# Two attention layers on one core: variances and row sums by quarters, 1 / sigma through DRAM, and a new order of the second layer's finish

## The chip, the cores and the metric

The kernel runs on one core of a Trainium2 chip. Its time is the device time of one execution in microseconds (us). The engines are TensorE (PE; PEld is its weight load), VectorE (DVE), ScalarE (ACT), GpSimd (POOL) and SyncE (SP), which here only issues DMAs. PE, DVE, ACT and POOL execute in the order in which the program names their instructions, and so does SP's queue.

## The reference

Everything is float32. The input x is [B, C, H, W] = [2, 512, 64, 32], so each batch has 2048 tokens of 512 channels.

```python
# layer 0: attention over all 2048 tokens, 8 heads of 64
q, k = concat(x, emb) @ Wq, concat(x, emb) @ Wk      # emb: 32 rows of frequency, 32 of time
v = x @ Wv
x = x + softmax(q k^T / 8) v @ Wout + bout

# layer 1: Nystrom attention with 256 landmarks, then a linear map
t = tokens(x)
q, k, v = split(layer_norm(t) @ Wqkv)
qL, kL = means of q / 8 and of k over 8 tokens each
attn1 = softmax(q kL^T); attn2 = softmax(qL kL^T); attn3 = softmax(qL k^T)
out = attn1 @ (pinv6(attn2) @ (attn3 @ v)) + conv33(v)   # pinv6: six steps of an iteration
t = t + out @ Wout1 + bout1
t = t + (layer_norm(t) @ nf4_weights^T) @ W^T            # the two maps become one matrix mT
```

`layer_norm` takes the mean and the variance over the 512 channels of each token, with no learned scale.

## The kernel before

Channels lie on the 128 partitions, tokens along the free axis, in four blocks of TB = 512 tokens per batch (`NTB` = 4); heads go in pairs (`NPAIR` = 4 per batch). A matmul of float32 is two instructions.

**Layer 0.** `Heads0` makes queries, keys and values of a pair. For the queries and keys it adds an embedding e, which for batch 0 is computed once on POOL (L889) and written to DRAM for batch 1. `attention0` runs the scores, exponentials, sums and values, and after each group of steps calls `advance` on a list of generators, the filler: the next pair's projections, and the finish of the batch before. A generator that yields `GAP` lets the others pass without having done anything; any other yield is a turn used. `finish0_units` is that finish for batch 0: it loads x, adds the output projection (`out0_units`), and normalizes (`norm0_steps`) for layer 1. Batch 1's finish runs by hand between the first projections of layer 1 (L1801 to L1825), with `others` as the work beside it. There `load_x`, the loads of `xr` (L1795), the stores of keys and queries (L1243) and the weights are all on SP's queue.

**A normalization.** `statistics` is a generator of four steps: the sum of the four channel blocks on DVE; the mean, by a matmul with a constant matrix `mean_w`, and the subtraction on DVE; squares on ACT and their sums on DVE; and the variance, again by a matmul with `mean_w` over all 512 columns (L1000), whose result is the same on all 128 partitions, and Sqrt on ACT. The caller takes the reciprocal over 128x512 on DVE (L1017, L1650) and multiplies.

**Layer 1.** `todo` holds eight pairs, batch 1's first. `attend` and `gram` make attn2 and its Gram matrix. For pair n, `pinv` runs the iteration; between its steps `chunk` (five times) and `last` (six times) are called, which emit pieces of other work: attn3 of the pair after (`attn3_scores`, `landmarks_values`, `start_values`), attn1 of the pair before (`attn1_scores`, `attn1_add`, `attn1_values`, `attn1_sums`, `attn1_inverse`, `attn1_end`), the values of the pair after the next, and `advance(finish)`. attn1's row sums are already made with 32 columns of ones at a time (`sums_of`, L779), each quarter of the partitions for another part of the columns; after a reciprocal over 256 columns, eight DMAs on SP (`spread`, L790) carry them to all columns. attn3's row sums use 64 columns of ones (L1406) and a reciprocal over 256 columns in place.

**The finish of layer 1.** `Finish1` is one block of it: x1 is loaded into `xb` by four DMAs on SP, `out_units` adds the output projection (yp_g, L965, with DVE's residual L972), `steps` or `norm_units` normalize, `map_units` applies mT (fp_g, L1682) and writes out. `finish1_units` strings together batch 1's four blocks on one `xb` buffer, 13 turns each; it is put on the list after pair 4 (`n == NPAIR`). After the last pair, `last_attn1` gives the rest of its attn1 in turns, and a string orders the turns: f is a turn of the finish, 1 one of `last_attn1`, a and b the output units of batch 0's blocks 0 and 1, s and t their normalization steps. Batch 0's four blocks `fs`, with their loads, are made ahead of the string. After it comes the bound's check (`halves`, `bp`, `ok`, `oks`, `bad`, L2051 to L2064), which tells whether the plain exponentials were safe, and then the loop over the last blocks.

[...]From layer 1's pairs on, `bank` has four of them (tag pp), before that two, beside two buffers of two banks each for scores (`scores_bank`).

Of the kernel before, what the change touches and what calls it, by code (L numbers as in the profile page):

```python
# [663 lines left out]
def fast_path(  # L664
# [108 lines left out]
    def sums_of(rs, acc):  # L773


        for h in range(2):
            for j in range(2):
                lo = h * D + j * Q
                nc.tensor.matmul(  # L779
                    rs[lo : lo + Q, :LM], lhsT=ones[:, :Q], rhs=acc[:, h, j * LM : (j + 1) * LM],  # L780
                    start=True, stop=True,
                )

    def spread(dst, few):

        for h in range(2):
            for to in range(2):
                for j in range(2):
                    lo, src = h * D + to * Q, h * D + j * Q
                    nc.sync.dma_start(dst[lo : lo + Q, j * LM : (j + 1) * LM], few[src : src + Q, :])  # L790
# [31 lines left out]
    nc.vector.memset(emb_sb, 0.0)  # L822
# [3 lines left out]
    def load_w0(kind, cols, queue=nc.sync):  # L826
        w = {"q": wq0, "k": wk0}[kind]
        nc.sync.dma_start(w_sb[kind][:, :, cols], chunked(w[:C, cols]))
        queue.dma_start(we[kind][:, cols], w[C:, cols])

    nc.gpsimd.dma_start(emb_sb[:32, :H], freq)
    nc.gpsimd.dma_start(emb_sb[32:, H:], time)
    load_w0("q", slice(0, P), nc.scalar)

# [23 lines left out]
    class Heads0:  # L858
# [12 lines left out]
        def embedded_and_projected(self, kind):  # L871

            cols, xbs = self.cols, self.xbs
            if kind == "q":
                self.q = qopool.tile([P, S], F32, tag="qo", name=f"q_{self.name}")

            def embedded(kind):


                e = wpool0.tile([P, H, W], F32, tag="e", name=f"e_{kind}_{self.name}")  # L880
                flat, kept = e.rearrange("p h w -> p (h w)"), e_d["qk".index(kind), self.hp]
                if self.b:
                    nc.sync.dma_start(flat, kept)
                    return flat
                fp = bank(f"fp_{kind}_{self.name}")
                nc.tensor.matmul(fp[:, : H + W], lhsT=we[kind][:, cols], rhs=emb_sb, start=True, stop=True)
                ft = wpool0.tile([P, H + W], F32, tag="ft", name=f"ft_{kind}_{self.name}")
                nc.vector.tensor_copy(ft, fp[:, : H + W])
                nc.gpsimd.tensor_tensor(  # L889
                    e,  # L890
                    ft[:, :H].unsqueeze(2).to_broadcast([P, H, W]),
                    ft[:, H:].unsqueeze(1).to_broadcast([P, H, W]),
                    ALU.add,
                )
                nc.sync.dma_start(kept, flat)
                return flat

            def project(kind, dst, e, t):
                toks = slice(t * TB, (t + 1) * TB)
                pp = bank(f"pp_{kind}_{self.name}_{t}")  # L900
                for k in range(KC):
                    nc.tensor.matmul(  # L902
                        pp, lhsT=w_sb[kind][:, k, cols], rhs=xbs[t][:, k, :], start=k == 0, stop=k == KC - 1
                    )
                nc.vector.tensor_tensor(dst[:, toks], pp, e[:, toks], ALU.add)  # L905

            dst = self.q if kind == "q" else self.k
            e = embedded(kind)
            if self.b:
                yield from gap(2)  # L910
            else:
                yield
                yield GAP
            for t in range(NTB):
                project(kind, dst, e, t)
                yield
# [63 lines left out]
    def statistics(xb, xn, part, name, squares, row):  # L980
# [12 lines left out]
        for i, other in enumerate(others):  # L993
            nc.scalar.activation(other, xn[:, 2 + i * n : 2 + (i + 1) * n, :], AF.Square)
            to = sq[:, i * n : (i + 1) * n, :]
            nc.vector.tensor_tensor(to, to, other, ALU.add)  # L996
        nc.vector.tensor_tensor(sq[:, 0, :], sq[:, 0, :], sq[:, 1, :], ALU.add)  # L997
        yield
        var = bank(f"var_{name}")
        nc.tensor.matmul(var, lhsT=mean_w, rhs=sq[:, 0, :], start=True, stop=True)  # L1000
        rstd = row()
        nc.scalar.activation(rstd, var, AF.Sqrt, bias=eps, scale=1.0)
# [7 lines left out]
    def norm0_steps(b, t, xb, xn, part):  # L1010
# [6 lines left out]
        nc.vector.reciprocal(rstd, rstd)  # L1017
# [8 lines left out]
    def finish0_units(b, oTs, outs_done):  # L1026
        last = None
        for t in range(NTB):
# [4 lines left out]
            for m, _ in enumerate(out0_units(b, t, xb, oTs)):  # L1033
                if last and m == 0:
                    next(last)
                yield
# [14 lines left out]
            yield  # L1051
        next(last)
# [155 lines left out]
    class Pair:  # L1208
# [59 lines left out]
        def attend(self):  # L1268

            i, L = self.i, self.L  # L1270
            scs = scores_bank(f"sc2_{i}") if i + 1 < NPAIR else None
            X = self.X = [zpool.tile([P, 2, LM + 1], F32, tag=f"M{h}", name=f"X_{i}_{h}") for h in range(2)]
            rs = small.tile([P, 4], F32, tag="rs2", name=f"rs2_{i}")
            for h in range(2):
                nc.gpsimd.memset(X[h][:, :, LM:], 1.0)
            for h in range(2):
                rows_h = slice(h * D, (h + 1) * D)
                sc = scs[:, h, :] if scs is not None else bank(f"sc2_{i}_{h}")
# [122 lines left out]
        def landmarks_values(self):  # L1401

            rs = bank(f"rs3_{self.name}")
            for j in range(2):
                for h in range(2):
                    nc.tensor.matmul(  # L1406
                        rs[h * D : (h + 1) * D, :LM],
                        lhsT=ones,
                        rhs=self.acc3[:, h, j * LM : (j + 1) * LM],
                        start=j == 0,  # L1410
                        stop=j == 1,
                    )
            rinv = self.acc3[:, 0, :]
            yT = rinv[:, LM:]
            nc.scalar.copy(rinv[:, :LM], rs[:, :LM])
            nc.vector.reciprocal(rinv[:, :LM], rinv[:, :LM])
            nc.vector.tensor_tensor(yT, self.av3[:, :LM], rinv[:, :LM], ALU.mult)
            X = exps(f"X2_{self.name}").rearrange("p a b -> p (a b)").rearrange("p (h k n) -> p h k n", h=2, k=2)
            self.X = [X[:, h] for h in range(2)]
            for h in range(2):  # L1420
                nc.sync.dma_start(self.X[h], X_d[self.b, self.hp, h])
            yield
# [205 lines left out]
    class Finish1:  # L1628
# [3 lines left out]
        def __init__(self, b, t, os, xb, xn):  # L1632
            self.b, self.t, self.os, self.xb, self.xn = b, t, os, xb, xn
            self.name = f"g_{b}_{t}"
            toks = slice(t * TB, (t + 1) * TB)
            for m in range(KC):
                nc.sync.dma_start(xb[:, m, :], chunked(x1_d[b])[:, m, toks])
# [4 lines left out]
        def steps(self, row):  # L1642
# [5 lines left out]
            for rstd in statistics(self.xb, self.xn, self.xn[:, :2, :], self.name, squares, row):  # L1648
                if rstd is not None:
                    nc.vector.reciprocal(rstd, rstd)  # L1650
                    self.rstd = rstd
                yield

        def norm_units(self):
            steps = self.steps(lambda: deviation(self.name))
            next(steps)
            yield GAP
            next(steps)
            yield
# [3 lines left out]
            yield  # L1663

# [27 lines left out]
    def finish1_units(b, os):  # L1692
        for t in range(NTB):
            xb = block_of(lpool, "xr", f"xb_g_{b}_{t}")
            f = Finish1(b, t, os, xb, lambda: block_of(lpool, "xn", f"xn_g_{b}_{t}"))
# [125 lines left out]
    advance(more)  # L1821
# [37 lines left out]
    def second_of_first():  # L1859
# [4 lines left out]
        for part in (landmarks, conv, landmarks, start, conv):  # L1864
# [20 lines left out]
    todo[1].prefetch_w()  # L1885
    vals = [values(1)]
    advance(vals)
    for n in todo[NPAIR - 1].front():
        advance(vals, n // 2)
    start_scale()  # L1890
    todo[0].prefetch1(kvpool.tile([P, S], F32, tag="k", name="q2_first"))
# [4 lines left out]
    for n, pair in enumerate(todo):  # L1896
# [20 lines left out]
        def chunk(c):  # L1917
            nonlocal landmarks
            if before and 0 < c <= n_ones:
                before.attn1_end(c - 1)  # L1920
            advance(finish)
# [35 lines left out]
        def last(i):  # L1957
            nonlocal start
            if i == 1 and after:
# [31 lines left out]
        if n == NPAIR:  # L1991
            finish.append(finish1_units(1, [p.o for p in todo[:NPAIR]]))

    def last_attn1():
        pair, ended = todo[-1], []
        for t in range(NTB):
            for j in range(2 if t else 0):
                pair.attn1_scores(t, j)
                if ended:
                    pair.attn1_end(ended.pop())  # L2000
                yield
            pair.attn1_add(t)
# [16 lines left out]
    fs = [last_block(t) for t in range(NTB)]  # L2019

# [5 lines left out]

    outs = [f.out_units() for f in fs]
# [9 lines left out]
    st = [f.steps(deviation_of(t)) for t, f in enumerate(fs)]  # L2037

    ones_last = last_attn1()
    for c in "f1f1f1f1f1f1f1fa1a1a1as11bs1bs1bbt":  # L2040
        if c == "f":
            advance(finish)
        else:
            next({"1": ones_last, "a": outs[0], "b": outs[1], "s": st[0], "t": st[1]}[c])
# [5 lines left out]

    n = 3 * B * NPAIR  # L2051

    halves = row_of("halves_f")[:, :P]
    nc.gpsimd.memset(halves, 0.0)
    nc.gpsimd.memset(halves[:D, :D], 1.0)
    nc.gpsimd.memset(halves[D:, D:], 1.0)
    bp = bank("bp_f")
    nc.tensor.matmul(bp[:, :n], lhsT=halves, rhs=bound, start=True, stop=True)
    ok = small.tile([P, n], F32, name="ok_f")
    nc.vector.tensor_scalar(ok, bp[:, :n], SAFE, None, ALU.is_lt)  # L2060
    oks = small.tile([P, 1], F32, name="oks_f")
    nc.vector.tensor_reduce(oks, ok, AX.X, ALU.min)
    nc.vector.tensor_scalar(oks, oks, -1.0, 1.0, ALU.mult, ALU.add)
    nc.gpsimd.partition_all_reduce(bad, oks, P, bass_isa.ReduceOp.max)  # L2064

# [99 lines left out]
```

## Time and profile before

| | us |
|---|---|
| median of 3 runs (lowest, highest) | 2764.85 (2764.79, 2766.75) |
| the profiled execution, its own time | 2763.73 |
| its span, first to last instruction | 2761.9 |
| PE busy in the span | 2703.8 |
| DVE, ACT, POOL busy | 1629.0, 905.8, 164.7 |

The mean granted clock of TensorE is 0.995 of full. The stages, with the busy time of PE in each, from the table of windows:

| us from the span's start | what | PE busy |
|---|---|---|
| 0 to 45 | loads, first projections | 40.7 |
| 45 to 1380 | layer 0's attention (finish of batch 0 within) | 1326.5 |
| 1380 to 1750 | finish of layer 0's batch 1, layer 1's keys and queries | 363.1 |
| 1750 to 2300 | pairs 0 to 5 | 548.2 |
| 2300 to 2590 | pairs 6 and 7 | 271.9 |
| 2590 to 2672 | rest of attn1, finish | 71.2 |
| 2672 to 2762 | last blocks | 82.1 |

A line of the profile names the engine, the line of the kernel, the operation, what it writes from what it reads, the shape and the count; busy time and idle time follow. In a timeline the first two numbers are the start and the length in us, and a bracket gives how long the engine had been idle before, and what it waited for.

### The profile page before, as it was taken

To read this page: it belongs to the slowest core of one execution; us is meant where nothing else is said; L and a number is where in the kernel's file an instruction comes from. 1 tells how busy PE (TensorE), PEld (TensorE's weight loads), DVE (VectorE), ACT (ScalarE), POOL (GpSimd) and SP (SyncE) were. 2 spreads that over 40 slices of the span, in tenths; PEclk is the share of its full clock that TensorE was granted. 3 is DMA by queue.
4 is the path that set the end of the run, shared out by engine and by line. 5 is a ranking of instruction groups with operands and counts; after the bars stand their busy time and mean duration, and the time that the engine had idled before them with its cause. 6 is when DMAs were issued, how large, how long until landed. Compare 5 with 4: busy or idle time off the path is not lost. (4 is left out here: it accounts for less than half of the span.)

```text
span 2761.9 us, 41236 instructions
## 1 busy us (share of the span) xinstructions
PE 2703.8 (98%) x16994; PEld 1363.3 (49%) x16994; DVE 1629.0 (59%) x2068; ACT 905.8 (33%) x1352; POOL 164.7 (6%) x125
## 2 busy tenths in 40 slices
PE   9999999999999999999999999999999999899898
PEld 5343443434443334343344465777667767555334
DVE  2768787765558756657657444544644545556465
ACT  1434343433335334344512222223332323221210
POOL 1101101000001100000011000000000000000000
PEclk9999999999999999999999999999999999999999
DMA  4100000212111210021035532213111202111301
GB/s 145 42 9 24 28 20 26 83 35 69 32 66 54 96 39 9 21 73 41 24 107 187 187 121 90 95 32 126 43 36 59 81 9 90 40 64 31 107 31 47
DMA packets 112661, 174.00 MB, mean 63 GB/s; under 512 B 16320, under 2 KB 68048, under 8 KB 107856
## 3 DMA queue, kind: packets, MB, share of 16 engines
q1 hardware_dynamic: 107968, 154.46, 17.3%
q0 software_dynamic: 4416, 16.79, 1.6%
q8 instruction: 135, 2.21, 0.3%
q14 instruction: 62, 0.51, 0.1%
q10 hardware_dynamic: 80, 0.03, 0.0%
HBM read 90.87 MB, written 63.57 MB: 56 GB/s over the span
## 5 line engine op out<-in xcount | busy, mean ns | idle before, releaser
L1084 DVE TENSOR_TENSOR acc_f<-acc_f,p_f 128x1024 f32<-128x1024 f32 x448 | 582.6, 1300 | 208.8 <-ACT p_f L1074 180.2
L1074 ACT ACTIVATE p_f<-sc_f 128x1024 f32<-128x1024 f32 x512 | 496.4, 1021 | 564.2 <-PE sc_f L1066 561.5
L1066 PE MATMUL sc_f<-q_f,k_f 64*64 64x512 f32 x4096 | 491.1, 594 | 2.7 <-ACT p_f L1074 2.7
L1096 PE MATMUL av_f<-p_f,v_f 64*64 64x512 f32 x4096 | 484.3, 589 | 0.0
L1096 PEld LDWEIGHTS av_f<-p_f,v_f 64*64 64x64 f32 x4096 | 156.5, 133 | 283.0 <-issue 283.0
L1066 PEld LDWEIGHTS sc_f<-q_f,k_f 64*64 64x64 f32 x4096 | 145.8, 133 | 285.6 <-issue 262.0
L1239 PE MATMUL pp<-xh,w 128*128 128x512 f32 x512 | 231.0, 603 | 0.7 <-ACT q L1242 0.7
L1239 PEld LDWEIGHTS pp<-xh,w 128*128 128x128 f32 x512 | 95.8, 192 | 122.2 <-issue 115.0
L1532 PE MATMUL pb<-R 128*128 128x192 f32 (+1 forms) x640 | 151.1, 383 | 1.6 <-DVE M L1545 1.6
L1532 PE MATMUL pa<-M 128*128 128x192 f32 (+1 forms) x640 | 150.7, 380 | 0.1
L950 PEld LDWEIGHTS vp_f<-wv_f,x 128*128 128x128 f32 x1024 | 115.7, 192 | 13.5 <-issue 11.8
L950 PE MATMUL vp<-w,xh 128*128 128x128 f32 x1024 | 120.8, 276 | 0.0
L950 PEld LDWEIGHTS vp<-w,xh 128*128 128x128 f32 x1024 | 117.0, 192 | 7.2 <-issue 4.2
L1532 PEld LDWEIGHTS pb<-R 128*128 128x128 f32 x640 | 107.7, 192 | 25.1 <-DVE M L1545 2.3
L950 PE MATMUL vp_f<-wv_f,x 128*128 128x128 f32 x1024 | 118.7, 277 | 0.0
L1532 PEld LDWEIGHTS pa<-M 128*128 128x128 f32 x640 | 108.0, 193 | 21.0 <-ACT M L1523 2.5
L902 PE MATMUL pp_q_f<-x,wq_f 128*128 128x512 f32 x256 | 114.4, 599 | 2.1 <-DVE q_f L905 1.4
L965 PE MATMUL yp_g<-o,wo_f 128*128 128x512 f32 x256 | 115.5, 598 | 0.8 <-DVE y_g L1671 0.8
L902 PE MATMUL pp_k_f<-x,wk_f 128*128 128x512 f32 x256 | 114.3, 599 | 1.7 <-DVE k_f L905 1.3
L1682 PE MATMUL fp_g<-xn_g,mT 128*128 128x512 f32 (+1 forms) x264 | 115.7, 589 | 0.0
L965 PE MATMUL yp_f<-q_f,wo_f 128*128 128x512 f32 x256 | 113.7, 598 | 0.9 <-DVE xr_f L972 0.9
L1114 POOL TENSOR_TENSOR q_f<-q_f,rinv_f 128x512 f32<-128x512 f32 x32 | 44.4, 1387 | 1041.9 <-DMA rinv_f<-acc_f 850.7
(196 smaller groups left out, 2719.3 us busy)
## 6 DMA issues: line engine op xcount, KB each, us to landing
xh<-xh_fd SPq DMA_DIRECT2D x12, 1024.0 KB, 5.6
rinv_f<-acc_f SPq DMA_DIRECT2D x256, 32.0 KB, 1.8
xr_f<-in_x_dram SPq DMA_DIRECT2D x8, 1024.0 KB, 5.2
x_fd<-xr_f POOLq DMA_DIRECT2D x8, 1024.0 KB, 5.0
xh_fd<-xn_f POOLq DMA_DIRECT2D x8, 1024.0 KB, 4.6
k_fd<-k SPq DMA_DIRECT2D x32, 256.0 KB, 2.6
q_fd<-q SPq DMA_DIRECT2D x32, 256.0 KB, 3.1
xb_g<-x_fd SPq DMA_DIRECT2D x32, 256.0 KB, 4.2
```

Of the source, the lines that this page charges most:

```text
L902: nc.tensor.matmul(pp, lhsT=w_sb[kind][:, k, cols], rhs=xbs[t][:, k, :], start=k == 0, stop=k == KC - 1)
L950: nc.tensor.matmul(vp[:, j * P : (j + 1) * P], lhsT=xb[:, k, j * P : (j + 1) * P], rhs=w_of(k), start=k == 0, stop=k == KC - 1,)
L965: nc.tensor.matmul(yp, lhsT=wo_sb[:, k, m * P : (m + 1) * P], rhs=oTs[k][:, toks], start=k == 0, stop=k == NPAIR - 1,)
L1066: nc.tensor.matmul(sc[r * D : (r + 1) * D, h, :], lhsT=hd.k[rows, lo : lo + D], rhs=hd.q[rows, t * TB : (t + 1) * TB], start=True, stop=True,)
L1074: nc.scalar.activation(p, sc, AF.Exp, scale=D**-0.5)
L1084: nc.vector.tensor_tensor(acc, first if c == 1 else acc, p, ALU.add)
L1096: nc.tensor.matmul(av[r][half, :], lhsT=hd.v[keys, c, half], rhs=pp[keys, h, :], start=c == 0, stop=c == NST - 1,)
L1114: nc.gpsimd.tensor_tensor(o, o, rinv, ALU.mult)
L1239: nc.tensor.matmul(pp, lhsT=self.w[j][:, c, :], rhs=xhs[t][:, c, :], start=c == 0, stop=c == KC - 1)
L1532: nc.tensor.matmul(dst, lhsT=lhsT[:, k, t * P : (t + 1) * P], rhs=rhs[:, k, :], start=k == 0, stop=k == 1)
L1682: nc.tensor.matmul(fp[:, cols], lhsT=mT[:, k, m * P : (m + 1) * P], rhs=self.xn[:, k, cols], start=k == 0, stop=k == KC - 1,)
```

## The change

**Statistics.** The variance is four matmuls of 128 columns each with 32 columns of `mean_w`, so quarter j of the partitions holds the variances of quarter j of the tokens. Sqrt and the reciprocal work on 128x128. One row of each quarter is written to DRAM (4 x 128) and read back to all partitions as 128x512, both on SP; the reciprocals in the callers go. `apart` puts a step between the squares on ACT and their sums on DVE. In `finish0_units` the multiplication (`next(last)`) moves from the next block's output unit 0 to unit 1, with two gaps ahead of the last one; in the finish by hand two turns instead of one stand ahead of the last.

**attn3's row sums.** `sums_of` takes a number of parts: two parts of 128 columns accumulate, and 128 columns of results are inverted and spread by eight DMAs. The product with the values becomes a step of its own, one step later, called from `last(0)`.

**Order.** Batch 1's finish is put on the list at pair 4's `chunk(1)`. A block of it takes 18 turns: its x1 comes by one DMA on POOL, with two gaps before its first unit; gaps stand behind the steps of its normalization. The string is new and has a letter n, at which batch 0's blocks are made and their 16 loads issued. `attn1_add` is emitted with the scores that it adds. The bound's check moves ahead of the pairs, around `start_scale`.

**Smaller ones.** The embedding's table loads and the first wq go to ACT's queue; the first pair's embedding is added on DVE instead of POOL; in `attend` the two heads' scores are two tiles (two buffers) instead of one, and the memset of ones is on DVE.

```diff
-    def sums_of(rs, acc):
-        for h in range(2):
-            for j in range(2):
-                lo = h * D + j * Q
-                nc.tensor.matmul(
-                    rs[lo : lo + Q, :LM], lhsT=ones[:, :Q], rhs=acc[:, h, j * LM : (j + 1) * LM],
-                    start=True, stop=True,
-                )
+    def sums_of(rs, acc, parts=1):
+        n = TB // parts // 2
+        for part in range(parts):
+            for h in range(2):
+                for j in range(2):
+                    lo, at = h * D + j * Q, part * 2 * n + j * n
+                    nc.tensor.matmul(
+                        rs[lo : lo + Q, :n], lhsT=ones[:, :Q], rhs=acc[:, h, at : at + n],
+                        start=part == 0, stop=part == parts - 1,
+                    )
...
     def load_w0(kind, cols, queue=nc.sync):
-        nc.sync.dma_start(w_sb[kind][:, :, cols], chunked(w[:C, cols]))
+        queue.dma_start(w_sb[kind][:, :, cols], chunked(w[:C, cols]))
...
-    nc.gpsimd.dma_start(emb_sb[:32, :H], freq)
-    nc.gpsimd.dma_start(emb_sb[32:, H:], time)
     load_w0("q", slice(0, P), nc.scalar)
+    nc.scalar.dma_start(emb_sb[:32, :H], freq)
+    nc.scalar.dma_start(emb_sb[32:, H:], time)
...
-                nc.gpsimd.tensor_tensor(
+                engine = nc.gpsimd if self.b or self.hp else nc.vector
+                engine.tensor_tensor(
...
+        if apart:
+            yield
+        for i, other in enumerate(others):
             to = sq[:, i * n : (i + 1) * n, :]
             nc.vector.tensor_tensor(to, to, other, ALU.add)
...
-        nc.tensor.matmul(var, lhsT=mean_w, rhs=sq[:, 0, :], start=True, stop=True)
+        for j in range(4):
+            nc.tensor.matmul(
+                var[j * Q : (j + 1) * Q, :P], lhsT=mean_w[:, :Q], rhs=sq[:, 0, j * P : (j + 1) * P],
+                start=True, stop=True,
+            )
+        few = sq[:, 1, :P]
+        nc.scalar.activation(few, var[:, :P], AF.Sqrt, bias=eps, scale=1.0)
+        nc.vector.reciprocal(few, few)
+        rstd_d = dram.tile([4, P], F32, name=f"rstd_d_{name}")
+        nc.sync.dma_start(rstd_d, few[::Q, :])
         rstd = row()
-        nc.scalar.activation(rstd, var, AF.Sqrt, bias=eps, scale=1.0)
+        nc.sync.dma_start(rstd, rstd_d.rearrange("j n -> (j n)").partition_broadcast(P))
...
-                if last and m == 0:
+                if last and m == 1:
                     next(last)
...
+        yield from gap(2)
         next(last)
...
-            scs = scores_bank(f"sc2_{i}") if i + 1 < NPAIR else None
+            scs = [scores_bank(f"sc2_{i}_{h}")[:, 0, :] for h in range(2)] if i + 1 < NPAIR else None
...
-            rinv = self.acc3[:, 0, :]
-            yT = rinv[:, LM:]
-            nc.scalar.copy(rinv[:, :LM], rs[:, :LM])
-            nc.vector.reciprocal(rinv[:, :LM], rinv[:, :LM])
-            nc.vector.tensor_tensor(yT, self.av3[:, :LM], rinv[:, :LM], ALU.mult)
+            sums_of(rs, self.acc3, 2)
+            few, rinv, yT = self.acc3[:, 0, :P], self.acc3[:, 0, LM:], self.acc3[:, 1, :LM]
+            nc.scalar.copy(few, rs[:, :P])
+            nc.vector.reciprocal(few, few)
+            spread(rinv, few)
...
+            yield
+            nc.vector.tensor_tensor(yT, self.av3[:, :LM], rinv, ALU.mult)
             yield
...
+            if t_by_t:
+                nc.gpsimd.dma_start(xb, chunked(x1_d[b])[:, :, toks])
+                return
             for m in range(KC):
                 nc.sync.dma_start(xb[:, m, :], chunked(x1_d[b])[:, m, toks])
...
         def norm_units(self):
-            steps = self.steps(lambda: deviation(self.name))
-            next(steps)
-            yield GAP
-            next(steps)
-            yield
+            steps = self.steps(lambda: deviation(self.name), True)
             next(steps)
             yield from gap(2)
             next(steps)
             yield
+            next(steps)
+            yield GAP
+            next(steps)
+            yield from gap(2)
+            next(steps)
+            yield
+            yield GAP
...
+            yield from gap(2)
             yield from f.out_units()
...
-    advance(more)
+    advance(more, 2)
     next(last)
...
+            if n == NPAIR and c == 1:
+                finish.append(finish1_units(1, [p.o for p in todo[:NPAIR]]))
...
         def last(i):
+            if i == 0 and after:
+                next(landmarks)
...
-        if n == NPAIR:
-            finish.append(finish1_units(1, [p.o for p in todo[:NPAIR]]))
...
+        pair.attn1_add(0)
         for t in range(NTB):
             for j in range(2 if t else 0):
                 pair.attn1_scores(t, j)
                 if ended:
                     pair.attn1_end(ended.pop())
+                if j:
+                    pair.attn1_add(t)
                 yield
-            pair.attn1_add(t)
             pair.attn1_values(t)
...
-    for c in "f1f1f1f1f1f1f1fa1a1a1as11bs1bs1bbt":
+    for c in "1f1fffffnf11f1ff1afaffff1f1f1f1faas11bs1bs1bbt":
         if c == "f":
             advance(finish)
+        elif c == "n":
+            fs = [last_block(t) for t in range(NTB)]
+            outs = [f.out_units() for f in fs]
+            st = [f.steps(deviation_of(t)) for t, f in enumerate(fs)]
```

The block of `halves`, `bp`, `ok`, `oks` and `bad` is the same text in its new place, ahead of `for n, pair in enumerate(todo)`; only `partition_all_reduce` of `bad` follows `start_scale`.

## The prediction

> **What bounds the kernel now.** I read the busy table first, then PE's waits, then the timeline round the longest of them, then the chain of waits at the end.
>
> ```profile
> PE 2703.8 (98%) x16994; PEld 1363.3 (49%) x16994; DVE 1629.0 (59%) x2068; ACT 905.8 (33%) x1352; POOL 164.7 (6%) x125
> ```
>
> TensorE is busy for all but 58 us of a span of 2761.9. So an edit pays in two ways only: fewer microseconds of matmul, or part of those 58 us. The five longest of PE's waits (total, times, longest):
>
> ```profile
> PE p_pb L1522 <- DVE R L1545: 7.2, 2, 6.8
> PE sc L1280 <- ACT X L1287: 6.2, 3, 3.5
> PE rs L779 <- DVE acc L1598: 5.1, 1, 5.1
> PE bp_f L2058 <- POOL halves_f L2056: 4.9, 1, 4.9
> PE mean_g L987 <- DVE xn_g L984: 3.0, 1, 3.0
> ```
>
> Four of them lie behind 2380 us, in the last two pairs and the stretch of `last_attn1`. The timeline tells what the 6.8 us one is:
>
> ```profile
> 2378.06 5.47 SPq L790 DMA_DIRECT2D rinv<-acc  x8
> 2386.12 1.75 SPq L1637 DMA_DIRECT2D xb_g<-x_fd  x4
> 2389.65 0.75 DVE L972 SCALAR_TENSOR_TENSOR xb_g<-yp_g,b_f,xb_g 128x512 f32<-128x512 f32 x1 [10.39 <-DMA xb_g<-x_fd]
> 2390.32 0.74 DVE L1545 SCALAR_TENSOR_TENSOR R<-M,pa 128x320 f32<-128x320 f32 x2
> 2390.85 0.48 PE L1522 MATMUL p_pb<-ident,R 128*128 128x128 f32 x1 [6.76 <-DVE R L1545]
> ```
>
> DVE stands at a residual whose block of x1 isn't loaded. SP issued eight spreads and the previous block's output ahead of that load, and the iteration of the inverse is queued behind DVE. A second loss follows every such wait: matmuls after it run slowly. In the chain at the end:
>
> ```profile
> 2614.80 0.61 PE rs L779 x8
> 2664.31 0.40 PE bp_f L2058 x2
> 2664.72 5.22 PE fp_g L1682 x8
> 2681.09 0.86 PE var_g L1000 x2
> ```
>
> Eight fp_g matmuls take 5.22 us after the wait for halves_f, and 3.43 to 3.63 elsewhere in that chain. The timeline shows the same after the other long waits: eight pp in 5.23 instead of 3.70 (1494), eight pb in 3.61 instead of 1.89 (2391), eight av in 3.48 instead of 1.94 (2524), rs and var in 3.1 instead of 1.5 (2597). That is 1.5 to 1.7 us on top of each wait of 3 us or more.
>
> **What the Trainium skill says.** "TensorE: Matmul & The Clock Gate", Part 1, has the array's clock halved after an idle window of about 3.4 us; the slow matmuls above agree. "TensorEngine Tiling (Array Packing)", Tiling Modes and Key Properties: 128x32 gives four tiles that work in parallel, and a change of mode drains the array. L779 agrees: eight instructions of 256 columns take 0.57 to 0.61 us together, against 0.43 for one full instruction of 512. "DMA: Bandwidth & Descriptors", Anatomy of one DMA, puts about 2 us fixed on a transfer; here the 32 KB spreads land 1.8 us after issue. "ScalarE: Activation LUTs", What ACT_TABLE_LOAD costs: 1283 ns, and 1283 is what L1002's loads show.
>
> **The change, part by part** (gains positive, us).
>
> *Variance by quarters.* Before, two instructions take 0.86 (chain). Now eight of 128 columns in quarters of the array. No row has that shape. Half of L779's 0.57 is the low end, 0.29; the whole of it the high end. The 128x64 convolution (88 instructions of up to 144 columns in 5.00, 57 ns each) gives 0.46. I take 0.42: 0.44 x 16 blocks = **+7.0** (4.6 to 9).
>
> *attn3's row sums.* L1406 holds PE for 0.91 (2301.26 to 2302.17). Sixteen instructions now, 0.57 to 0.91, taken as 0.70: 0.2 x 8 = **+1.7** (0 to 2.7). It adds eight spread DMAs to SP per pair, 64 in all, at 0.62 us of issue (4.95 / 8), and DVE waits for them before yT: 0.4 copy + 0.95 reciprocal + 5 issue + 1.8 = 8.2 us. Behind that DVE wait is the start vector's R. Cover: convolution 5.0, flips and product 1.8, values 3.8, so 10.6 of PE work. Little is left over if SP is late.
>
> *1 / sigma.* The reciprocal of 128x512 (3351 ns; 1752 for 256) becomes one of 128 columns, about 0.95 by that slope; Sqrt falls from 0.69 to 0.37. DVE loses 2.4 x 16 = 38 us of work, nearly all off the path. In return comes a write and, after its landing, a read on SP: 32 DMAs. Sqrt 0.4, reciprocal 0.95, twice (0.5 issue + 2 landing): 6.4 us from variance to 1 / sigma, plus 1.28 with a table load. Consumers by stage:
> - Tail (2670 on): the wait is covered by 13.7 us of yp and 3.4 of fp, in the last block by 3.4 of fp and four banks. Nothing.
> - `finish0_units` inside attention: a turn is 7 us or more, so "a turn later" covers it. In the drain at 900 to 925 turns are short, and the next xr load is queued on SP behind the round trip (and waits for xr's own quarter to be written out): that load moves from 899.9 to about 904.5. There 2.3 us of PE waits stood; removing the 3.34 reciprocal helps, the late load costs about 4: **-2**.
> - Layer 1's start (1400 to 1475), three transitions: the reciprocal now stands ahead of the next block's part sum on DVE and waits for table load and Sqrt, so the mean is late by 0.2 to 1.4; and the xr load, issued at 1428.87, goes behind the round trip to about 1434, landing near 1440 where the residual used it at 1436.6. The second pp bank hides 2.5 of the 3.5. About 1.7 each: **-5** (0 to -9).
>
> *Two score banks in `attend`.* The 6.2 us and one slow clock (1.5) go; the next pp then meets an ACT queue with the exponentials in it. I take **+6.5** (4 to 7.7).
>
> *Head.* PE waits 0.61, 0.94, 0.40 and 1.33 before 35 us, for x and for POOL's embeddings (3.63 each; a DVE tensor_tensor of 2048 is 2.28 at L988). The second embedding must still wait for the first one's store, which is in the DMA backlog until 29 us. **+1.6** (0.5 to 2.5).
>
> *Finish of batch 1 from pair 4 on, x1 by one POOL load, two gaps behind it, Squares and their adds a turn apart, and the new order.* A block takes 18 turns instead of 13, 20 more in all; 10 come from pair 4, 11 from the string (19 f against 8). The load has two turns before its residual and no SP spreads ahead; POOL pays one issue (0.79) and may stand for the old block's output to land, with only `attn1_end`'s additions behind it. SP's spreads and outputs stand behind each block's round trip for 2 to 3 us, inside a turn. What can go: the 6.8 us wait with its followers, 7.2 + 1.7 of clock, **+8** (5 to 8.9). Eleven short waits between 2440 and 2590 sum to 9.6, + 1.5 of clock; pair 7 keeps a filler at each of `last`'s six places, but loses four yp or fp units to the string. **+6** (2 to 10). `attn1_add` is put next to its scores and the adds apart from the squares: the 5.1 us wait + 1.6, **+6** (3 to 6.7).
>
> *halves and bad moved to before the pairs.* There POOL and its row are free; three DVE instructions of 0.15 are in front of the scale, beside matmuls of `values`. At the end 4.95 + 1.6 go, and 0.8 at 2625: **+7** (5 to 7.3).
>
> *New waits* in the late order: the last blocks' 16 loads (4 MB) now stand on SP at "n", about 10 us of issue, ahead of a spread and of block 3's round trip. By PE's work in between (21 us until both are used) they arrive 2 us early. With the attn3 spreads I take **-4** (0 to -10).
>
> Sum: 7.0 + 1.7 - 2 - 5 + 6.5 + 1.6 + 8 + 6 + 6 + 7 - 4 = 32.8. The profiled execution took 2763.73 (span 2761.9 and 1.8 around it): 2730.9. The runs' median, 2764.85, is 1.1 above it: **2732**.
>
> **Rivals.**
> 1. *Waits move on.* DVE and SP stay strict queues, and breaking one wait puts the next in its place. Of the three late items (20) only a third stays, the rest as forecast: 2732 + 13 = 2745; with new waits at their worst, 2751. For it: before has eleven short waits there from changing causes. Against: the longest have one cause each that the edits remove. Chance 0.24.
> 2. *Quarters don't shorten.* Drains at two mode changes eat the gain: 8.7 less, 2741. Against it: L779 already runs at that shape. 0.08.
> 3. *The round trip is on the path: slower.* Without its costs the gains sum to 40. If DVE stands at 1 / sigma with the residuals or the attention sums behind it, and SP with the x loads behind it, PE loses e per block: 16 e beats 40 from e = 2.5. At e = 3.2, half of the 6.4, it is 51 - 40 = 11 slower: 2776. For it: the layer-1 start shows DMA busy up to 0.9 of a slice, and the read always waits out the write. Against: only seven or eight of the 16 blocks have covers under 10 us. 0.06.
> 4. *It doesn't do what it says* (the order keeps the finish at its old pace): then only the edits outside the order pay, 16.8, less the 4 of new waits: 2752. 0.02.
>
> **Numbers.** The forecast has 0.60. All upper ends without losses give some 2710; 2716 to 2754 holds rivals 1 and 2 and leaves out rival 3 and the extremes. A measurement of this kernel can tell about 0.2%, 5.5 us, from no change. Faster 0.91 (forecast, 1, 2 and most of 4), same 0.03, slower 0.06.
>
> **What would show it.** var rows of 128x128 with 32-column tiles, x128, about 0.42 a block in the chain. PE's waits for halves_f and for ACT X gone; no wait over 3 us behind 2300; xb_g loaded once by POOL before its residual. DVE's reciprocals shorter by some 46 us with attn3's. PE busy lower by about 9 plus the slow-clock time, idle from 58 to about 35. In 1400 to 1475 PE waits for mean_n or for xr: there the round trip costs. Wrong, if PE idles at y_g's rstd or at residuals in attention, or if the late idle stays over 20 us.

## The result and the profile after

The changed kernel takes 2758.31 us (median of 7 runs, 2755.31 to 2760.09) against 2765.75 for the kernel before (7 runs): a ratio of 0.9969, 95% interval 0.9958 to 0.9981. It is 7.4 us faster where 33 were forecast, and it lies outside the range. The profiled execution took 2758.68, its span 2756.9, which is 5.0 shorter than the one profiled before.

The busy table of after, and PE's waits (total, times, longest):

```profile
PE 2693.9 (98%) x17154; PEld 1360.1 (49%) x17154; DVE 1579.9 (57%) x2087; ACT 899.6 (33%) x1352; POOL 152.7 (6%) x109
```

```profile
PE yp_f L972 <- DVE xr_f L979: 7.0, 3, 5.5
PE pa L1545 <- ACT M L1536: 6.9, 2, 5.4
PE wp L1520 <- DVE R L1558: 5.9, 3, 2.4
PE rs_f L782 <- DVE acc_f L1104: 5.2, 4, 2.3
PE wp L1520 <- ACT M L1536: 4.6, 1, 4.6
PE wp L1520 <- ACT o L1484: 4.3, 1, 4.3
PE fp_g L1700 <- DVE rinv L1638: 3.7, 1, 3.7
```

M, R, wp, pa and pb belong to the iteration of `pinv`. The five waits of the list before (p_pb for R, sc for X, rs for acc, bp_f for halves_f, mean_g for xn_g) are gone. Of the seven that stand there now, four are new (both for M, o, and rinv), and three have grown: yp_f from 0.9, wp for R from 2.4, rs_f from 3.0. PE's busy time fell by 9.9 us, but its idle time rose from 58.1 to 63.0. Behind 2300 it is idle for 30.5 us (36.7 before): the prediction's own sign of being wrong, over 20 there, came true. The same instructions in both traces divide the span; the forecast's terms are sorted into the same stretches (us, negative is shorter):

| from, to | before | after | measured | forecast |
|---|---|---|---|---|
| start, first yp_f | 711.8 | 709.9 | -1.9 | -1.6 |
| first yp_f, first pp of layer 1's keys | 569.0 | 575.9 | +6.9 | +0.2 |
| first pp, last pr | 458.2 | 449.5 | -8.7 | -3.2 |
| last pr, end | 1022.9 | 1021.6 | -1.3 | -28.2 |

In the third row the forecast is four quarters (-1.75), the round trip (+5) and the two score banks (-6.5); in the last row it is eight quarters (-3.5), attn3's sums (-1.7), halves (-7) and the late order (-20 + 4). So 27 us are missing behind 1735 and 7 between 710 and 1286, and between 1286 and 1735 the kernel gained 5.5 more than forecast.

### The profile page after: what moved, and what is told of

It is laid out like the page before. It is cut to its first block, busy times and chain, and to the rows that moved or that the text cites. A ratio compares the mean times of both kernels' runs of the same rounds, so it can differ in the third digit from the quotient of the medians.

```text
span 2756.9 us, 41707 instructions
## 1 busy us (share of the span) xinstructions
PE 2693.9 (98%) x17154; PEld 1360.1 (49%) x17154; DVE 1579.9 (57%) x2087; ACT 899.6 (33%) x1352; POOL 152.7 (6%) x109
## 4 chain that ended last, share of the span: by engine, by line
PE 89%; DVE 5%; DMA 2%; ACT 1%; SPq 1%; issue 1%; DVEq 0%; ACTq 0%
PE sc_f L1086 15%; PE av_f L1116 14%; PE pp L1259 8%; PE pa L1545 5%; PE pb L1545 5%; PE vp L957 4%; PE vp_f L957 4%; PE fp_g L1700 4%; PE pp_k_f L909 4%; PE yp_g L972 3%; PE yp_f L972 3%; PE pp_q_f L909 3%; DVE acc_f L1104 2%; PE av L1402 2%; PE sc L1602 2%; PE sc L1381 2%
```

## The experiments

Twelve kernels, in three groups. Ratios are to the kernel before, whose median was 2766.43, 2767.26 and 2766.85 in the three groups. Differences to after are differences of medians; beside after the kernel before took 2765.75, so a difference of 1 to 2 us to after can't be told from none.

**First: one edit to after each.** The convolution's stores:

```diff
-                    nc.sync.dma_start(o_d[self.b, self.hp][:, toks], row)
+                    nc.gpsimd.dma_start(o_d[self.b, self.hp][:, toks], row)
```

> The kernel after with one line changed: the convolution's rows of pairs that are stored (o_d) go out through POOL's queue instead of SP's. Theory A (SP's order): in pairs 5 and 6 these stores stand on SP behind attn3's eight spreads, so the ring of three rows is freed late, ACT's copy of o waits (5.21 and 4.54), the flips of M behind it too, and PE waits 4.55 and 4.29 for wp, each followed by about 2 us of slow matmuls. Off SP, both waits go: 9 to 12 us less. Rival B (waits move on): the flips are late anyway, because DVE waits for the same spreads before yT and R; then 0 to 3 us less.

Measured: 2744.94, ratio 0.9926 (0.9912 to 0.9939), 13.4 less than after. The timeline of after where PE waits for M the first time:

```profile
2195.65 5.47 SPq L794 DMA_DIRECT2D acc<-acc  x8
...
2201.22 1.51 SPq L1485 DMA_DIRECT2D o_fd<-o  x3
...
2203.90 0.59 ACT L1484 COPY o<-cv 128x512 f32<-128x512 f32 x1 [5.21 <-DMA o_fd<-o]
2204.38 0.44 ACT L1536 COPY M<-tp_M 128x128 f32<-128x128 f32 x2
...
2204.71 1.28 PE L1520 MATMUL wp<-M 128*64 128x256 f32 x4 [4.55 <-ACT M L1536]
...
2205.92 5.37 PE L957 MATMUL vp<-w,xh 128*128 128x128 f32 x32
```

and the same place with the stores on POOL:

```profile
2195.69 5.77 SPq L794 DMA_DIRECT2D acc<-acc  x8
2196.50 0.58 POOL L1485 DMA_DIRECT2D o_fd<-o  x1 [3.28 <-ACT o L1484]
...
2199.33 0.59 ACT L1484 COPY o<-cv 128x512 f32<-128x512 f32 x1 [0.61 <-PE cv L1472]
2199.54 1.41 PE L1520 MATMUL wp<-M 128*64 128x256 f32 x8
...
2200.88 3.84 PE L957 MATMUL vp<-w,xh 128*128 128x128 f32 x32
```

Read it from the top. attn3's eight new spreads hold SP for 5.47 us. The convolution's stores were ready from 2196 on but stand behind them. The ring of rows has three, so the fourth copy on ACT waits for a store, the two flips of M (PE transposes M into tp_M, ACT copies it back) wait behind that copy, and PE waits for the flips. With POOL issuing the stores the copy comes 4.57 earlier, and the vp matmuls behind it take 3.84 instead of 5.37. DVE's product with the spread values is no sooner (2203.47 against 2202.63), and PE doesn't need it then: rival B falls. Over the whole span PE's idle time fell by 8.8 (63.0 to 54.2) and its busy time by 7.9, more slow-clock time than I had reckoned; this execution was the fastest of the five.

The banks of the last maps:

```diff
-        return product_bank(name) if m % 2 else side_bank(1 + m, name)
+        return product_bank(name) if m % 2 else side_bank(3 - m, name)
```

> The kernel after with the two even banks of the last maps exchanged, so that the first map no longer takes the bank that the last attn1_end reads. Theory A (a second wait lay under the one for halves): fp_g's 3.7 us wait for DVE rinv and the 2.9 us of slow fp_g after it go, 5 to 7 us less. Rival B: the map then waits for y_g's xn instead (DVE has the same additions ahead of it), 0 to 2 us less.

Measured: 2751.87, ratio 0.9950 (0.9937 to 0.9964), 6.4 less than after; the wait for rinv is off the list. Theory A. In the timeline of after the map stood behind the last `attn1_end`, and that behind a landing spread:

```profile
2653.89 4.95 SPq L794 DMA_DIRECT2D rinv<-acc  x8
...
2660.27 0.69 DVE L1638 TENSOR_TENSOR rinv<-av,rinv 128x512 f32<-128x512 f32 x1 [0.42 <-DMA rinv<-acc]
...
2661.11 6.38 PE L1700 MATMUL fp_g<-xn_g,mT 128*128 128x512 f32 x8 [3.68 <-DVE rinv L1638]
```

The fp_g matmuls don't read rinv. They write the bank (of PSUM, where matmuls put their results) that `attn1_end` reads last.

The squares in batch 1's norm, with the number of turns kept:

```diff
             yield                 # behind mean and subtraction
+            yield GAP
             next(steps)           # squares
             yield GAP
             next(steps)           # adds
-            yield from gap(2)
+            yield GAP
             next(steps)           # variance
```

> The kernel after with the turns inside a block's norm in batch 1 placed differently, as many as before: the squares one call later behind the mean, the adds still a call behind the squares, the variance one call sooner behind the adds. Theory A (ACT is a strict queue): the squares no longer stand on ACT ahead of the flip while DVE's subtraction is late; PE's waits for ACT M (5.44 at 2541 and 1.43 at 2240) go with about 2 us of slow matmuls, 5 to 9 us less. Rival B (waits move on): the variance comes sooner behind the adds and PE waits for sq, or the squares meet another flip; then between 2 us less and 5 us more.

Measured: 2751.79, ratio 0.9951 (0.9937 to 0.9964), 6.5 less than after. Both waits for M behind pa are gone; the wait of var_g for sq_g is 2.9 where it was 1.5, so a little did move on. What stood there, from the timeline of after:

```profile
2535.95 0.69 DVE L1638 TENSOR_TENSOR rinv<-av,rinv 128x512 f32<-128x512 f32 x1 [1.59 <-DMA rinv<-acc]
2536.56 2.28 DVE L995 TENSOR_TENSOR xn_g<-xb_g,mean_g 128x2048 f32<-128x2048 f32 x1
...
2538.87 1.06 ACT L998 ACTIVATE sq_g<-xn_g 128x1024 f32<-128x1024 f32 x1 [6.67 <-DVE xn_g L995]
...
2540.87 0.24 ACT L1536 COPY M<-p_pa 128x128 f32<-128x128 f32 x1
2541.17 1.44 PE L1545 MATMUL pa<-M 128*128 128x320 f32 x2 [5.44 <-ACT M L1536]
...
2542.61 3.62 PE L1545 MATMUL pa<-M 128*128 128x192 f32 x8
```

Three strict queues pass one delay on: DVE waits 1.59 for a spread and then subtracts for 2.28; the squares stand at the head of ACT's queue all that time (6.67); the flip of 0.24 us that PE needs is behind them. The pa that follow take 3.62 instead of 1.89.

Layer 0's blocks back on chip (the rest of after kept):

```diff
         var = bank(f"var_{name}")
+        if local:
+            nc.tensor.matmul(var, lhsT=mean_w, rhs=sq[:, 0, :], start=True, stop=True)
+            rstd = row()
+            nc.scalar.activation(rstd, var, AF.Sqrt, bias=eps, scale=1.0)
+            yield rstd
+            return
...
-        for rstd in statistics(xb, xn, part, name, squares, lambda: deviation(name)):
+        for rstd in statistics(xb, xn, part, name, squares, lambda: deviation(name), local=True):
             yield
+        nc.vector.reciprocal(rstd, rstd)
```

> The kernel after with layer 0's eight blocks back to one full variance (two instructions of 0.43), Sqrt and reciprocal of 128x512 on chip, no transfer of 1 / sigma. Theory A (the round trip costs more in layer 0 than its quarters gain): the stage from 712 to 1281 loses some 6 us of PE waits and the layer-1 start 3, while the variances cost 8 x 0.43 = 3.5 more and the reciprocal on DVE a part of its 3.35 in the drain: 2 to 6 us less in all. Rival B (the added waits there come from the moved turns, not from the transfer): the waits stay, and it is 2 to 4 us more by the variances alone.

Measured (c4_norm0_local): 2763.45, ratio 0.9988 (0.9981 to 0.9994), 5.1 more than after: theory A missed. The 5.5 us wait for yp_f is gone, but one of 4.4 for mean_n stands in its place. This run alone can't tell whether the round trip costs anything, because the change had also moved the turns at which the steps are called, and this run kept them moved. A later run puts them back.

**Second: layer 0's queue, all four together, and halves alone.** The round trip's two DMAs by `nc.gpsimd` instead of `nc.sync` in layer 0:

> The kernel after with layer 0's round trip of 1 / sigma kept, but its write and its read issued by POOL's queue instead of SP's. Theory A (SP's order): the load of the next xr no longer stands behind the round trip, so in the drain at 900 us it is issued some 5 us sooner; PE's 5.5 us wait for yp_f there goes with 1.8 us of slow yp: 4 to 7.5 us less. Rival B (the moved turns): with layer 0's round trip taken out altogether another wait of 4.4 us stood in the same place, so the wait comes back as one for mean or var: 0 to 2 us less.

Measured: 2756.00, ratio 0.9960 (0.9946 to 0.9973), 2.3 less than after. PE still waits 4.3 at the same residual. The load of xr is no longer behind the round trip in SP's queue, and still it goes out as late as in after: 5.5 us behind the variance (901.57 against 896.11). SP's order is not what holds it here.

The stores on POOL, the bank swap, the squares' gap and this edit in one kernel:

> The kernel after with four edits together: convolution's stores on POOL, the two even banks of the last maps exchanged, the squares a call later, layer 0's round trip on POOL. Theory A (separate waits in separate places): their gains add: 13.4 + 6.4 + 6.5 and 0 to 7 for the last, so 2725 to 2733. Rival B (waits move on): each wait that goes lets the next one in the same stretch grow, less than two thirds of the sum stays: over 2740.

Measured: 2731.16, ratio 0.9865 (0.9850 to 0.9880), 27.2 less than after. The four single gains sum to 28.6. So the waits are separate, and taking one away brought hardly another up: that of var_g for sq_g, 1.5 in after, is 2.9 here.

The block of halves, bp and bad moved in the kernel before, with nothing else:

> The kernel before with one edit of the change alone: the block of halves, bp and bad moved to before the pairs. Theory A (a doubly covered wait): DVE's last attn1_end releases the bank of the first map 2 us before halves comes, so the 4.9 us wait becomes one for rinv of about 3: 2 to 3.5 us less. Rival B (the prediction's term): the wait goes whole with its slow matmuls, 6 to 7.3 us less.

Measured: 2767.82, ratio 0.9998 (0.9990 to 1.0007): no gain that the times show, and rival B's 6 to 7.3 is out. Theory A's 2 is just within the interval. The timeline:

```profile
2666.56 0.69 DVE L1625 TENSOR_TENSOR rinv<-av,rinv 128x512 f32<-128x512 f32 x1 [0.35 <-DMA rinv<-acc]
...
2667.40 5.37 PE L1682 MATMUL fp_g<-xn_g,mT 128*128 128x512 f32 x8 [3.11 <-DVE rinv L1625]
```

The wait of 4.95 for halves_f became one of 3.11 for rinv, with the same 5.37 of slow fp_g behind it. From var_g to the first fp_g it is 2.1 us shorter (4.13 against 6.22). This execution was 4.9 behind the profiled one of before at var_g already, 2.5 of it at the last pr, which stands ahead of the moved block; executions of the kernel before differ by up to 6.2. The same with the bank swap added:

> The kernel before with the block of halves moved to before the pairs and, besides, the two even banks of the last maps exchanged. Theory A (a doubly covered wait): now both covers are off, 5 to 8 us less than before, some 3 to 5 more than with the block moved alone. Rival B (the bank is no cover): the same as with the block moved alone.

Measured: 2760.13, ratio 0.9975 (0.9966 to 0.9985), 7.1 less than before. With both releases out of the way the first map follows var_g without a wait, and its eight fp_g take 3.60. The bank swap alone in the kernel before was not run.

**Third: the two banks alone, and the rest of layer 0.** In the kernel before, one score bank for each head in `attend`, as the change has it:

> The kernel before with one edit of the change alone: a score bank for each head in attend, instead of one tile of both. Theory A (the prediction's term): PE's three waits for ACT X, 6.2 in all, and the slow pp after the longest go: 4 to 7.7 us less. Rival B (waits move on): the projection behind meets ACT busy with the exponentials and waits for its bank instead: 0 to 3 us less.

Measured: 2760.11, ratio 0.9977 (0.9968 to 0.9985), 6.7 less than before. The prediction had 6.5, and the three waits for ACT X are gone. But the gain doesn't come from where theory A looks for it. The place of the longest of the three in before:

```profile
1488.49 1.13 PE L1280 MATMUL sc<-L,L 64*128 64x256 f32 x4
1493.09 1.24 PE L1280 MATMUL sc<-L,L 64*128 64x256 f32 x4 [3.47 <-ACT X L1287]
...
1503.76 3.10 PE L1307 MATMUL pr<-X 128*128 128x257 f32 x16
```

and with the two banks:

```profile
1487.54 1.14 PE L1280 MATMUL sc<-L,L 64*128 64x256 f32 x8
...
1495.20 0.69 DVE L997 TENSOR_TENSOR xr_f<-xr_f 128x512 f32<-128x512 f32 x1
...
1496.00 2.05 PE L1000 MATMUL var_n<-xr_f,mean_w 128*128 128x512 f32 x2 [3.69 <-issue]
1497.84 5.33 PE L1239 MATMUL pp<-xh,w 128*128 128x512 f32 x8
...
1503.01 3.10 PE L1307 MATMUL pr<-X 128*128 128x257 f32 x16
```

PE stands 3.69 us at the variance instead, which starts as DVE's sum of the squares ends ("issue" says only that the profile names no releaser), and the slow matmuls come behind that wait. From the first sc to pr it takes 15.5 us against 15.3: here the wait moved on. The gain lies at the wait of 2.0 (sc at 1527.67 to pr at 1540.49: 12.8 before, 8.0 now) and, with 1.2, ahead of 1488.

Layer 0 on chip again, now with its turns put back too:

```diff
-                if last and m == 1:
+                if last and m == 0:
...
-        yield from gap(2)
         next(last)

     def attention0(hd, filler, n_filler, needed, beside=None, every=False):
```

> The kernel after with all of layer 0's part undone: one full variance, Sqrt and reciprocal on chip as in the run named c4_norm0_local, and also the turns at which the steps are called put back. Theory A (the turns were chosen for the transfer, and with the reciprocal on chip they do harm): the 4.4 us wait for mean_n of that run and the 2.3 at 1092 go, the stage from 712 to 1281 is back at 569 from 578.5, in all 2753 to 2757, 7 to 10 us less than that run, and so layer 0's whole part of the change gained nothing. Rival B (the waits come from elsewhere): 0 to 3 us less than that run, over 2760.

Measured: 2753.43, ratio 0.9956 (0.9942 to 0.9970): 10.0 less than with the new turns, and 4.9 less than after. From first yp_f to first pp it takes 569.1, as before (569.0). PE's waits between 711 and 1287 in it:

```profile
PE mean_n L994 <- DVE xn_f L991: 1.4, 1, 1.4
PE sc_f L1092 <- ACT p_f L1100: 1.3, 3, 0.7
PE yp_f L972 <- DVE xr_f L979: 0.9, 1, 0.9
```

These are the waits of the kernel before. So in layer 0 the change lost 4.9 us net, its quarters included: by the stretches it lost 6.8 from first yp_f to first pp and won 2.8 from there to the last pr (452.3 here, 449.5 in after).

The quarters of 1 / sigma out of the block of x, POOL's queue kept:

```diff
-        few = sq[:, 1, :P]
+        rstd = row()
+        few = rstd[:, :P] if queue else sq[:, 1, :P]
```

> The kernel after with layer 0's round trip on POOL's queue, and the quarters of 1 / sigma no longer in the block of x but in the row that the read fills later. Theory A (a buffer, not SP's order): the next xr load waits for the write of the quarters because they lie in its block; now it waits only for the variance's matmuls and goes out 5 us sooner, at 896.5: PE's 4.3 us wait left in the run with POOL's queue alone goes with 1.7 of slow yp, 4 to 8 us less than after. Rival B (the load is late for another reason): 1 to 3 us less, as with POOL's queue alone.

Measured: 2755.47, ratio 0.9962 (0.9949 to 0.9976), 2.8 less than after: by the time, rival B's figure. By the stretch it is theory A: first yp_f to first pp takes 570.6, 5.3 less than after. The head of this profiled execution was 3.6 longer. The timeline of after, with the load behind both DMAs:

```profile
895.41 0.43 PE L1012 MATMUL var_n<-xr_f,mean_w 128*32 128x128 f32 x8
...
898.79 0.53 SPq L1020 DMA_DIRECT2D rstd_d_n<-xr_f  x1
...
900.43 0.33 SPq L1022 DMA_DIRECT2D rstd_n<-rstd_d_n  x1
...
900.92 0.39 SPq L1049 DMA_DIRECT2D xr_f<-in_x_dram  x1
...
907.63 1.41 DVE L979 SCALAR_TENSOR_TENSOR xr_f<-yp_f,b_f,xr_f 128x512 f32<-128x512 f32 x2 [8.87 <-DMA xr_f<-in_x_dram]
908.43 8.94 PE L972 MATMUL yp_f<-q_f,wo_f 128*128 128x512 f32 x16 [5.54 <-DVE xr_f L979]
```

and with the quarters in the row:

```profile
898.99 0.43 PE L1012 MATMUL var_n<-xr_f,mean_w 128*32 128x128 f32 x8
...
899.51 0.37 SPq L1050 DMA_DIRECT2D xr_f<-in_x_dram  x1
...
904.49 0.75 DVE L979 SCALAR_TENSOR_TENSOR xr_f<-yp_f,b_f,xr_f 128x512 f32<-128x512 f32 x1 [2.15 <-DMA xr_f<-in_x_dram]
```

The load goes out 0.5 us behind the variance instead of 5.5, and PE's wait for yp_f is gone; 2.5 for mean_n is left. With POOL's queue it was a buffer that held the load: the quarters lay in the block that it overwrites. In after SP's order stands beside it, as the read goes out only 0.5 ahead of the load. The row with SP's queue kept was not run; by this timeline alone it would free the load little.

Last, the four edits with this one, and with the variance three calls behind the adds again:

> The four edits together once more, with the quarters in the row of 1 / sigma instead of the block of x, and in batch 1's norm the variance again three calls behind the adds (the call saved at its end). Theory A: on top of 2731.2, the 2.9 us wait of var for sq and the 4.2 of yp_f go with 1.7 of slow clock: 2722 to 2727. Rival B: the map's first rest then comes before 1 / sigma has landed and DVE stands there: 2728 to 2735.

Measured: 2723.08, ratio 0.9848 (0.9835 to 0.9862), 35 us less than after and 44 less than before: faster than both kernels. Its busy table and PE's largest waits:

```profile
PE 2682.3 (99%) x17154; PEld 1355.6 (50%) x17154; DVE 1582.7 (58%) x2087; ACT 899.5 (33%) x1352; POOL 173.6 (6%) x133
```

```profile
PE rs_f L782 <- DVE acc_f L1105: 5.2, 4, 2.3
PE p_pa L1536 <- DVE M L1510: 3.3, 2, 2.1
PE var_g L1012 <- DVE sq_g L1007: 2.9, 1, 2.9
PE mean_n L994 <- DVE xn_f L991: 2.5, 1, 2.5
```

No wait reaches 3 us. That of var_g for sq_g stayed at 2.9, so the earlier variance was not its cause.

## Why the prediction was wrong, point by point

- **Variance by quarters**, +7.0: about right, though not the same everywhere. The 0.42 or 0.43 of the timelines has the last matmul's modelled end in it; in the chain, where the 0.86 stood, a block takes 0.36. In the last blocks the yp_g behind it take 13.93 instead of 13.73, so 0.3 is won there. In layer 0's attention, where matmuls of 64*64 stand on both sides, it is 0.7 (var_n to the next sc_f: 1.06 before, at 781.61, and 0.36, at 779.71). So rival 2's cost at the change of shape is there in the last blocks, but it doesn't eat the gain.
- **attn3's sums**, +1.7: PE's part was low. The sixteen instructions take 0.57 (from 2193.58, the next work starting at 2194.15) against 0.91, 2.7 in all. What was wrong is the sentence on cover. It asked whether DVE's wait for the spreads delays PE. At the two long waits it does not. SP's queue behind the spreads does, through o's stores, the ring of three rows and ACT's flips: 13.4. I had counted the spreads on SP and had not listed what else SP issues in that stretch.
- **1 / sigma in the drain**, -2: the place was right and the size wrong. The stretch grew by 6.9 although the four quarters took some 1.75 off it (0.44 each, as forecast), so it cost about 8.6. The load's delay was forecast well (4.6; it goes out 5.5 behind the variance instead of 1.2). But the residual had been 0.9 late before, so every microsecond of that delay went to PE: 5.5 of wait and 1.8 of clock, against waits of 0.9 and 1.4 that went. The help from the shorter reciprocal, which I had set at 2, was not there. I had named both the queue and the buffer, and priced them as one. The round trip was also longer than the 5.0 of its two transfers: 6.2 from the write's issue (898.79) to the multiplication (904.99). In the run with POOL's queue the write of 2 KB lands in 1.7 us, near the 2 that were taken (the section cited for them is on transfers that GpSimd issues), and the read, 256 KB to all partitions, in 5.6 (medians). The moved turns also left DVE late for the row sums at 1092, another 2.3 and its clock; with the turns put back that wait is gone.
- **1 / sigma at layer 1's start**, -5: the wrong way. From first pp to last pr after is 2.8 faster than the kernel with layer 0 undone. The waits that were feared are there, seven between 1400 and 1510, none over 1.2, 4.1 in all. But the other kernel has as much: 3.7 for var_n in one wait (it is the one that the two banks brought up), with eight pp in 5.29 instead of 3.70 behind it, and 0.4. That slow time and the quarters make the difference. Why var_n no longer waits in after, the reciprocal of 3.35 that is gone from DVE ahead of it or the added turn, is not shown.
- **Two score banks**, +6.5: the number is right (6.7 alone), the working is not, and that is luck. The wait of 3.5 and its slow clock, 5.0 of the term's 7.7, paid nothing alone, as the wait moved on to var_n. The wait of 2.0 paid 4.8, because it too had slow matmuls behind it, for which the term had nothing.
- **Head**, +1.6: not shown. First av_f starts at 57.1 in after and at 59.0 in before, but from 57.7 to 61.4 in the nine other profiles of kernels with the same head.
- **halves**, +7: the step that failed most simply. It took the whole wait of 4.95 and its slow matmuls as saved. Alone it gave 2.1 in its stretch and nothing that the times show, as the bank was released only 2 us before halves_f. The list gives a wait's length down to its last release; what goes when that release comes early is only the distance to the second last. The bank, 6.4 in after, is that second last.
- **Late order**, +20, and **new waits**, -4: this is the step that failed in size. From last pr to the end the kernel gained 1.3. Three waits cost 13.4 + 6.5 + 6.4 = 26.3 as measured one by one. With them out (the kernel with four edits) the stretch takes 994.1, 28.8 less than before, where the terms without the new waits sum to 32.2. So the 6.8, the 5.1 and the short waits largely paid as forecast, together; none was run alone. The 4 for new waits was the bad number: it should have been 20, 13.4 for SP's order and 6.5 for the squares on ACT.

Rival 1 (waits move on) was the nearest in what happened, and its 2751 was still too low a price. Its mechanism is only half right: the new waits were not the next ones in line behind the old. The one for the bank was, and with the two banks alone that for var_n. Those of SP and ACT were made by the change itself, which put spreads, squares and subtractions at new places in strict queues. The 7 us that are left are the sum of large gains and large losses. Rival 3's mechanism, the round trip on the path, made layer 0's part, with its moved turns, a loss of 4.9 and not the whole change. Rival 4's 2752 is near by number alone: the new order does what it says.

## What to carry to other kernels

When an instruction is added to a queue, list what stands behind it there and which buffer that work frees. Follow it to the engine that bounds the kernel: here eight small DMAs on SP reached TensorE through a store, a ring of three rows and a copy on ACT. Before a wait is counted as saved, find the release that came second last, for the operands and for the bank that is written, and look whether the next instruction will wait as long. A new value that is put into a block with free columns prolongs that block's life until it has been written out: with POOL's queue the load into that block went out at 901.57, 1.8 behind the write and just ahead of the read.

## What had not been expected of the hardware

The prediction set the loss of clock at waits of 3 us or more. Some shorter ones cost it too. The table of windows of after around a wait of 2.28 us (start and end, length, then busy time and instructions of PE, PEld, DVE, ACT and POOL, then the granted clock, DMA share and GB/s):

```profile
1090.00:1093.00 3.00, 0.72 (x12) 0.16 (x8) 2.89 (x3) 0.58 (x1) 0.00 (x0) 1.00 0.00 0
1093.00:1094.00 1.00, 1.00 (x12) 0.30 (x8) 0.75 (x2) 0.00 (x0) 0.00 (x0) 0.50 0.00 0
1094.00:1096.00 2.00, 2.00 (x16) 0.49 (x8) 1.16 (x1) 0.66 (x1) 0.00 (x0) 0.50 0.00 0
```

The clock is 0.50 for the 3 us that follow. In the fastest kernel a wait of 2.86, from 2579.87 to 2582.73, left it at 1.00:

```profile
2579.00:2582.00 3.00, 0.87 (x3) 0.04 (x1) 2.06 (x4) 0.00 (x0) 0.00 (x0) 1.00 0.22 52
2582.70:2584.00 1.30, 1.27 (x10) 0.67 (x11) 0.00 (x0) 0.76 (x1) 0.00 (x0) 1.00 0.00 0
```

"TensorE: Matmul & The Clock Gate", Part 1, in the Trainium skill, has the clock fall after an idle window of about 3.4 us of a free-running count. A free-running count fits that 2.28 lost it and 2.86 didn't; that waits below 3.4 lose it at all does not follow from it, and here they did, the 3.0 for mean_g in the prediction's list, with eight av in 3.48 instead of 1.94 behind it, among them. A single wait of some 4.5 us, with the slow matmuls behind it, was worth 6.7 in the run with the stores on POOL (13.4 for two).
